# A time-mix layer with a GELU FFN on one core: the first loads in a written order, and the last block's tiles in earlier chunks

## The chip, the cores and the metric

The kernel runs on one core of a Trainium2 chip. The metric is the time in microseconds that the device takes for one execution; shorter is better. The core has engines that run side by side and wait for each other by semaphores: TensorE (PE in the profile, with its weight loads as PEld), VectorE (DVE), ScalarE (ACT), GpSimd (POOL) and SyncE (SP). SP computes nothing; its queue issues most of the kernel's DMAs. ACT can issue DMAs too, in the same queue as its own work.

## The reference

The input is x with 4 sequences of 1024 tokens of 512 channels. It is normalised, and the sum of x, a time-mix branch and an FFN branch is the output.

```python
xn = _layernorm(x)
# time mix
xx = concatenate([xn[:, 1:2, :], xn[:, :-1, :]], axis=1) - xn
k = einsum('btc,hc->bth', xn + xx * time_mix_k, Wk)      # HIDDEN = 704
r = einsum('btc,hc->bth', xn + xx * time_mix_r, Wr)
w = exp(-exp(time_decay))
state = state * w + relu(k_t);  out_t = state * r_t      # scan over t
out = einsum('bth,ch->btc', out, Wv)
out = (out - mean) * rsqrt(var + 1e-5) * ln_gamma + ln_beta
# FFN, N = 2048
D = gelu(dot(fp16(xn), W0.T) + bias0)                    # rounded to fp16
E = fp16(dot(D, W1.T) + bias1)
return x + out + E
```

## The kernel before, in words

The tokens are cut into 8 blocks of 512 (two to a sequence). A block is computed channel-major: `xnT` holds the transposed normalised block, and one tile is 128 partitions by 512.

*Precision.* Products that have to be near float32 are made of several passes in the fast float32 format: an operand is split into a truncated part, a rest, and a mixture (`split_x`, L281, `split_kr`, L238). Three passes with a scale S make one product (`three_pass`, L624): 8 matmuls into a bank `pa`, 4 into a bank `pb`, then ACT scales `pa` (L642), and DVE adds `pb` (L643). HIDDEN is 5 tiles of 128 and a half tile of 64 (`half_pass`, L653). Block 0, whose weights are still being split, uses plain float32 products (`raw_k`, `raw_r`, `raw_halves`).

*A block's loop.* For each block i, n runs over the 16 chunks of 128 rows of the FFN's hidden dimension N. A turn of n does, in PE's order: `up` for chunk n + 2 (L782, 8 matmuls, bank `pd`), `down` for chunk n (L810, 8 matmuls into the four accumulators `pe`, one for each row tile s of 128 tokens), and then the time-mix tiles that the dictionary `pieces` holds for that n. The work on ACT and DVE that follows a tile (relu, the scan over time, the gate with r, the splits of the gated result, the norm of an output tile) is run as a "follower" in the turn after it, woven with the background jobs `bg[n]` (weight fetches, splits, the next block's norm and transposes). For the blocks from 1 on, the five k tiles stand in chunks 0 to 4, the two halves in 5 and 6, the five r tiles in 7 to 11, and the four output tiles (`out_piece`, from the gated result and Wv) in 12 to 15. In the last block, the output tiles stand two to a chunk in 12 and 13 instead. The order of the PE, DVE, ACT and SP instructions within this loop is the written one (`manual_schedule`); elsewhere a planner of the framework orders the instructions.

*The last block's end.* There the down groups of the last 4 chunks (`tail = 4`) are left out of the loop. After the loop they are run for each row tile s by itself: tiles 0 and 1 into `pe` (L1022), tiles 2 and 3 by halves of the columns into fresh banks `end` (`end_by_columns`, L820), for which the sums of chunks 0 to 11 plus the bias have been put into `base` (L1016). Each is followed by a rounding (L769), an addition to the residual (L775) and a store of the output (L779).

*Weights and buffers.* Terms of Wk and Wr are written to DRAM once and fetched for each tile (`load_kr`, L275, three loads of 256 KB, name `kr`; 6 buffers, so two tiles' worth). W1's terms (`w`, 512 KB, 2 buffers) and W0's low terms (`w0l`, 256 KB, 3 buffers) are fetched for each chunk. All of these are on SP's queue, in the written order, where a load waits until its buffer is free. Most other tiles come from one common pool of 62 buffers (tag `q`), small scratch tiles from a ring of 6 (`temp`), PE's results from 4 banks (`bank`) and 4 more for `pe`.

*The start.* `load_x` (L100) issues the four row tiles of x's first block on SP, and the first three tiles of Wk in the middle of them (`amid`). ACT's queue issues the small loads: the two mix vectors (`mix_rows`), the decay in two parts and the FFN's bias (`late_rows`, 22 rows that are transposed on PE and become per-partition scalars). Three tiles of Wr follow on SP. These first loads are ordered by the planner. DVE clears a part of `late_rows` (L134), and the loads of its full rows come behind that. `first_inputs` (L389) then works out the first block by row tiles: the statistics and a square root on ACT (L416) for tile 0, the normalisation (L309), the transposes on PE (`turned`, L429), the mixing (`mixed_first`), and the first products (L387) of k. In PE's written order, the transpose of `mix_rows` (L462) comes behind 10 dummy products (L405) and ahead of the first transposes; the transpose of `late_rows` (L467) and one more dummy product stand between the first transposes and the first products.

Of the kernel before, what the change touches and what calls it, by code (L numbers as in the profile page):

```python
# [22 lines left out]
def time_mix_and_gelu_ffn(  # L23
# [69 lines left out]
    def bank(name):  # L93
        return ps_mm.tile([P, TB], F32, tag="mm", name=name)
# [2 lines left out]
        b, t0 = blocks[i]  # L97
        return b, slice(t0 + s * P, t0 + (s + 1) * P)

    def load_x(i, name, amid=lambda: None):  # L100
        xs = const.tile([P, NS, C], F32, tag="x", name=f"{name}_{i}")
        for s in range(NS):
            if s == NS // 2:
                amid()
            b, rows = tokens_of(i, s)
            nc.sync.dma_start(xs[:, s, :], x[b, rows, :])
        return xs
# [9 lines left out]
        src = sources[kind].rearrange("(c p) k -> p c k", p=P)  # L117
        nc.sync.dma_start(raw_w[kind, h], src[:, :, h * P : (h + 1) * P])

    x_now = load_x(0, "x", lambda: [load_raw(0, h) for h in range(FIRST)])  # L120
    ident = part("ident", F32)[:, :P]
    make_identity(nc, ident)
    nhalf = const.tile([P, NS], F32, name="nhalf")
# [7 lines left out]
    mk_sb, mr_sb = mix_sb[:, :NC], mix_sb[:, NC:]  # L131
    ND = NF + 1
    late_rows = part("late_rows", F32)[: ND + NN, :P]
    nc.vector.memset(late_rows[:, HF:], 0.0)  # L134
    late_sb = const.tile([P, ND + NN], F32, name="late_sb")
    w_sb, b0_sb = late_sb[:, :ND], late_sb[:, ND:]

    def rows_of(ap):
        return ap.rearrange("(c p) -> c p", p=P)

    nc.scalar.dma_start(mix_rows[:NC], rows_of(mix_k))
    nc.scalar.dma_start(mix_rows[NC:], rows_of(mix_r))
    nc.scalar.dma_start(late_rows[:NF], rows_of(decay[:H0]))
    nc.scalar.dma_start(late_rows[NF:ND, :HF], decay[H0:].rearrange("(c p) -> c p", p=HF))
    nc.scalar.dma_start(late_rows[ND:], rows_of(bias0))
    for h in range(FIRST):
        load_raw(1, h)
    raw_half = part("raw_half", F32).rearrange("p (two c k) -> p two c k", two=2, c=NC)
    gamma_sb = const.tile([P, C], F32, name="gamma_sb")
    beta_sb = const.tile([P, C], F32, name="beta_sb")  # L150
# [442 lines left out]

        return after

    def raw_halves(j, sums):
        for c in range(NC):
            for q, sum_ in enumerate(sums):
                rows = slice(q * HF, (q + 1) * HF)
                for out_, kind, src in (  # L600
                    (sum_[:HF], 0, xks[j, c]),
                    (sum_[HF:], 1, xrs[j, c]),
                ):
                    nc.tensor.matmul(  # L604
                        out_,
                        raw_half[rows, kind, c, :],
                        src[rows],
                        start=(c == 0),
                        stop=(c == NC - 1),
                    )  # L610

        def after():
            both = temp(f"kr_{j}")
            nc.scalar.copy(both, sums[0])
            nc.vector.tensor_add(both, both, sums[1])
            rk, st = temp(f"rk_{j}_{NF}"), temp(f"st_{j}_{NF}")
            nc.scalar.activation(rk[:HF], both[:HF], AF.Relu)
            yield
            scanned(j, NF, HF, st, rk)
            yield from gated_half(j, st, both[HF:])  # L620

        return after
# [250 lines left out]
    with tc.manual_schedule(engines=engines):  # L873
        for i in range(len(blocks)):
            j = i + 1
            tail = 4 if i == LAST else 0
            by_columns = range(NS // 2, NS) if tail else ()
            pieces, bg, early = {}, defaultdict(list), defaultdict(list)

            def put(n, fn, *args):  # L880
                bg[n].append(lambda: fn(*args))
# [14 lines left out]
            def turn(first, end):  # L896
                transposed(state["x"], first, end)

            for s in range(NS):
                pieces[12 + (s // 2 if i == LAST else s), s] = [out_piece, i, s]  # L900
            if i == 0:
                state["x"] = x_next
                pieces[1, 0] = [raw_k, i, 3]
                pieces[3, 0] = [raw_r, i, 3]
                pieces[5, 0] = [raw_k, i, 4]
                pieces[7, 0] = [raw_r, i, 4]
                pieces[9, 0] = [
                    lambda i: raw_halves(i, [bank(f"pkr_{i}_{q}") for q in range(2)]), i
                ]
                put(0, several, split_kr, (1, 0, 0), (1, 1, 0))  # L910
                put(0, several, split_w0, (1, 2), (1, 3))
                for c in range(NC):
                    put(2 + c - (c == 0), split_w0, 2, c)
                    put(3 + c, load_w0, 3, c)
                    put(5 + c, split_w0, 3, c)
                put(1, stats, *range(NS))
                put(3, lambda: norm_apply(j, state["x"]))
                for n, *which in ((1, 0, 1), (3, 0, 2), (5, 0, 3), (7, 0, 4), (7, 1, 1)):
                    put(n, split_kr, 1, *which)
                put(4, turn, 0, 1)  # L920
                put(5, turn, 1, 5)
                put(7, turn, 5, 10)
                put(8, turn, 10, 11)
                put(9, turn, 11, 16)
                put(9, load_late_constants)
                put(12, split_half)
                mix_at = (11, 12, 13, 15)
            else:
                order = [(0, h) for h in range(NF)] + [(1, h) for h in range(NF)]
                for k, (kind, h) in enumerate(order):  # L930
                    pieces[k + 2 * kind, 0] = [three_pass, i, kind, h]
                    if k > 1:
                        split_here = (kind, h) in raw_w
                        put(k - 2 + 2 * (k > 6) + split_here, fetch_kr, i, kind, h)
                pieces[5, 0] = [half_pass, i, 0]
                pieces[6, 0] = [half_pass, i, 1]
                for c, n in enumerate((2, 3, 4, 5) if i == 1 else (2, 2, 3, 3)):
                    put(n, split_xr, i, c)
                if j <= LAST:
                    put(1 if i == 1 else 2, fetch_x)  # L940
                    for s in range(NS):
                        put(2 + s // 2 if i == 1 else 4, stats, s)
                    put(4 if i == 1 else 5, lambda: norm_apply(j, state["x"]))
                    turns = (4, 6, 4, 2) if i == 1 else (4, 5, 4, 3)
                    for k in range(sum(turns)):
                        unit = next(n for n in range(4) if k < sum(turns[: n + 1]))
                        put(6 + unit, turn, k, k + 1)
                mix_at = (10, 12, 13, 15) if i == 1 else (10, 12, 13, 14)
            if i == 1:
                for g in range(NN // G):  # L950
                    put(4 * g, store_w0l, g)
                for h, n in enumerate((11, 12, 13, 13, 13, 15)):
                    put(n, split_wv, h)
            put(11 if j <= LAST else 2, fetch_residual)
            if j <= LAST:
                for c in range(NC):
# [9 lines left out]
            for n in range(NN):  # L966
                ahead = n + AHEAD
                if ahead == NN and j <= LAST:
                    xf = next_xf
                nxt = (i, ahead) if ahead < NN else (j, ahead - NN)  # L970
                gelu = up(*nxt) if nxt[0] <= LAST else None
                works = [follow() for follow in followers]
                works = [w for w in works if next(w, works) is None]
                several(scaled_now, *early[n])
                if i == 0 or n == NN - NS or (n > NN - NS and i < RAW_OUT):
                    finished(*works)
                    works = []
                followers = []
                if gelu:
                    d = gelu()  # L980
                if ahead + 1 == NN and j <= LAST:
                    next_xf = ffn_input(j)
                if n < NN - tail:
                    operands = waiting.pop(0)
                    for s in range(NS):
                        down(n, s, *operands, end=NN - tail if s in by_columns else NN)
                if gelu and i > 0:
                    waiting.append((d, load_w1(*nxt)))
                two_on = (i, ahead + 2) if ahead + 2 < NN else (j, ahead + 2 - NN)
                if two_on[0] <= LAST:  # L990
                    load_w0l(*two_on)
                jobs = [
                    lambda s=s: finish(i - 1, s, e16s[s])
                    for s in (2 * n, 2 * n + 1)
                    if s < len(e16s)
                ]
                for s in range(NS):
                    if (n, s) in pieces:
                        fn, *args = pieces[n, s]
                        followers.append(fn(*args))  # L1000
                if i == 0 and ahead + 1 < NN:
                    load_w1_raw(ahead + 1)
                woven(works, jobs + bg[n])
                if i == 0:
                    waiting.append((d, load_w1(*nxt)))
                store_weights()
# [60 lines left out]
```

## Time and profile before

| | us |
|---|---|
| median of 3 runs | 873.87 |
| lowest, highest | 873.59, 874.65 |
| the profiled execution's own time | 874.32 |
| span in its profile, from the first to the last instruction | 872.5 |
| PE busy | 861.3 |
| DVE busy | 669.7 |
| ACT busy | 431.1 |
| mean granted clock of TensorE | 0.997 |
| DMA, mean rate over the span | 225 GB/s |

The profile is of one execution. Its times count from the first instruction. A line of the timeline gives the start, the duration, the engine, the line of the program, the operation, and the result and operands; "x3" means that several like instructions are merged. The bracket at the end tells how long the engine had been idle and which instruction or DMA released it. An engine's name with a q (SPq, ACTq) is its queue, which issues DMAs; a DMA's duration there is that of the issue, and its landing is some microseconds later.

### The profile page before, as it was taken

What the parts mean: (1) busy time and instruction counts of PE and PEld (TensorE: products, weight loads), DVE (VectorE), ACT (ScalarE), POOL (GpSimd) and SP (SyncE); (2) the same over time, 40 slices, a digit from 0 to 9 for tenths busy, and PEclk for the clock granted to TensorE, in tenths of its full rate; (3) what the DMA queues carried; (4) which work ended last, traced back from release to release, by engine and by line L of the source; (5) the groups of instructions that cost most, each with busy time, mean ns of one, the idle gap of its engine ahead of it and who ended that gap; (6) DMA issues with size and microseconds to landing.
All of it is one profiled execution on the core that took longest, in us unless ns stands there. A gap on an engine that the chain in (4) does not pass through costs nothing.

```text
span 872.5 us, 11125 instructions
## 1 busy us (share of the span) xinstructions
PE 861.3 (99%) x3760; PEld 687.6 (79%) x3760; DVE 669.7 (77%) x1098; ACT 431.1 (49%) x733; POOL 73.8 (8%) x142
## 2 busy tenths in 40 slices
PE   8999999999999999999999999999999999999996
PEld 7677657887578888888888888888888888888885
DVE  4778876798777978778887888788886797864547
ACT  3866643456634464445625356254553446444430
POOL 1100000000011001000021001100011200200001
PEclk9999999999999999999999999999999999999998
DMA  8687946957568655877559666696756866577631
GB/s 261 224 279 264 335 169 207 313 173 254 184 223 276 224 186 181 287 243 236 177 171 335 208 214 198 208 320 205 223 195 218 306 192 226 181 234 280 232 122 50
DMA packets 101029, 196.59 MB, mean 225 GB/s; under 512 B 11087, under 2 KB 25452, under 8 KB 100972
## 3 DMA queue, kind: packets, MB, share of 16 engines
q1 hardware_dynamic: 100912, 195.86, 67.5%
q8 instruction: 30, 0.49, 0.2%
q14 instruction: 27, 0.22, 0.1%
q10 hardware_dynamic: 60, 0.02, 0.0%
HBM read 167.00 MB, written 28.84 MB: 224 GB/s over the span
## 4 chain that ended last, share of the span: by engine, by line
PE 97%; DVE 1%; DMA 1%; issue 0%; SPq 0%; ACTq 0%; ACT 0%; DVEq 0%
PE pd L790 27%; PE pe L812 26%; PE pa L630 15%; PE pb L387 7%; PE oa L727 6%; PE po L686 4%; PE ob L735 3%; PE ph L659 3%; PE pk L387 2%; PE pr L387 2%; PE ob L737 1%; DMA wk<-in_L_attn_Wk 1%; PE po L698 0%; PE pkr L604 0%; DVE xres L775 0%; PE pt L429 0%
## 5 line engine op out<-in xcount | busy, mean ns | idle before, releaser
L812 PE MATMUL pe<-w,d 128*128 128x512 f32 x1008 | 248.9, 389 | 0.0
L812 PEld LDWEIGHTS pe<-w,d 128*128 128x128 f32 x1008 | 189.1, 188 | 39.5
L790 PE MATMUL pd<-xf,w0h 128*128 128x512 f32 x512 | 203.5, 398 | 0.0
L790 PE MATMUL pd<-xf,w0l 128*128 128x512 f32 x512 | 199.3, 389 | 0.0
L800 ACT ACTIVATE d<-pd,late_sb 128x512 f16<-128x512 f32 x128 | 87.7, 685 | 161.5 <-PE pd L790 161.3
L790 PEld LDWEIGHTS pd<-xf,w0h 128*128 128x128 f32 x512 | 96.1, 188 | 25.8 <-issue 4.9
L790 PEld LDWEIGHTS pd<-xf,w0l 128*128 128x128 f32 x512 | 96.2, 188 | 21.7 <-issue 1.9
L643 DVE SCALAR_TENSOR_TENSOR y<-pb,a 128x512 f32<-128x512 f32 x70 | 48.4, 691 | 70.5 <-PE pb L387 69.5
L642 ACT ACTIVATE a<-pa 128x512 f32<-128x512 f32 x70 | 41.9, 598 | 86.3 <-PE pa L630 86.0
L805 ACT CAST d<-d 128x512 fp32r<-128x512 f16 x128 | 79.6, 622 | 4.0
L331 DVE STREAM_TRANSPOSE xnT<-x 32x512 f32<-32x512 f32 x112 | 78.6, 702 | 2.1
L630 PE MATMUL pa<-hk,kr 128*128 128x512 f32 x140 | 54.5, 389 | 0.0
L630 PE MATMUL pa<-lk,kr 128*128 128x512 f32 x140 | 54.5, 389 | 0.0
L299 POOL TENSOR_SCALAR ry<-mvy 128x1 f32<-128x1 f32 x32 | 16.5, 514 | 436.9 <-DVE mvy L306 436.9
L630 PE MATMUL pa<-hr,kr 128*128 128x512 f32 x128 | 49.8, 389 | 0.0
L630 PE MATMUL pa<-lr,kr 128*128 128x512 f32 x128 | 49.8, 389 | 0.0
L727 PE MATMUL oa<-wv,hg 128*128 128x512 f32 x120 | 46.7, 389 | 0.0
L727 PE MATMUL oa<-wv,lg 128*128 128x512 f32 x120 | 46.7, 389 | 0.0
L645 ACT ACTIVATE y<-y 128x512 f32<-128x512 f32 x35 | 22.2, 633 | 47.6 <-DVE y L643 47.6
L387 PE MATMUL pb<-mk,kr 128*128 128x512 f32 x140 | 37.4, 389 | 0.0
L686 PE MATMUL po<-wvraw,g 128*128 128x512 f32 x80 | 35.6, 592 | 0.0
L387 PE MATMUL pb<-mr,kr 128*128 128x512 f32 x128 | 34.2, 389 | 0.0
(166 smaller groups left out, 1322.3 us busy)
## 6 DMA issues: line engine op xcount, KB each, us to landing
w<-w1d SPq DMA_DIRECT2D x110, 512.0 KB, 3.7
kr<-krd SPq DMA_DIRECT2D x201, 256.0 KB, 4.9
w0l<-w0d SPq DMA_DIRECT2D x96, 256.0 KB, 4.3
x<-in_L_attn_x SPq DMA_DIRECT2D x32, 256.0 KB, 5.3
w1d<-w SPq DMA_DIRECT2D x16, 512.0 KB, 3.0
xres<-in_L_attn_x SPq DMA_DIRECT2D x32, 256.0 KB, 5.3
krd<-wt SPq DMA_DIRECT2D x30, 256.0 KB, 3.9
out<-xres SPq DMA_DIRECT2D x28, 256.0 KB, 5.2
```

What stands on the lines that cost most here:

```text
L331: nc.vector.transpose(dst[i * Q : (i + 1) * Q, :, :, j, :], src[j * Q : (j + 1) * Q, :, :, i, :],)
L387: return nc.tensor.matmul(dst, w[:, c, :], src, start=(c == 0), stop=(c == NC - 1))
L630: nc.tensor.matmul(pa, w[p][:, c, :], xs[j, c][p], start=(c == 0 and p == 0), stop=(c == NC - 1 and p == 1),)
L642: nc.scalar.activation(a, pa, AF.Copy, scale=1.0 + 1.0 / S)
L643: nc.vector.scalar_tensor_tensor(y, pb, -1.0 / S, a, ALU.mult, ALU.add)
L659: nc.tensor.matmul(pa, w[:, c].rearrange("p two k -> p (two k)"), xs[j, c][p], start=(c == 0 and p == 0), stop=(c == NC - 1 and p == 1),)
L686: nc.tensor.matmul(pos[s], gs[i, h][:, s * P : (s + 1) * P], wv_raw[h], start=(h == 0), stop=False,)
L727: nc.tensor.matmul(pa, gs[i, h][p][:, cols], wv[h][p], start=(h == 0 and p == 0), stop=(h == NF - 1 and p == 1),)
L790: nc.tensor.matmul(pd, w, xf[c], start=(c == 0 and p == 0), stop=(c == NC - 1 and p == 1),)
L800: nc.scalar.activation(d16, pd, AF.Gelu, bias=b0_sb[:, n : n + 1])
L805: nc.scalar.copy(d, d16)
L812: nc.tensor.matmul(pe[s] if sum_ is None else sum_, d[:, s * P : (s + 1) * P], w1[p][:, cols], start=(n == first and p == 0), stop=(n == e ...
```

## The change

There are two parts.

*The loads.* The order of the first loads on SP and ACT is now a written one. ACT's queue keeps the two mix loads and has them first. The decay and bias loads go to SP's queue. `load_x` takes one list of loads for each row tile, which are issued ahead of that tile: SP's order is x tiles 0 and 1, three tiles of Wk, x tile 2, the three small row loads, x tile 3, three tiles of Wr. `late_rows` is cleared by GpSimd instead of VectorE.

*The last block.* The k, r, half and output tiles get their chunks from lists. For the last block, the k tiles move from chunks 0, 1, 2, 3, 4 to 0, 1, 2, 2, 3, the halves from 5, 6 to 3, 4, the r tiles from 7 to 11 to 4 to 8, and the output tiles from 12, 12, 13, 13 to 9, 10, 11, 11. The fetch of the weights' terms for tile k stays right behind tile k - 2, wherever that is; the splits of the r input move from chunks 2, 2, 3, 3 to 1, 2, 2, 3. In chunks 12 and 13 only `up` for chunks 14 and 15 is left. A chunk's entry in `pieces` may now hold several works. For the other blocks the lists give the same chunks as before.

```diff
-    def load_x(i, name, amid=lambda: None):
+    def load_x(i, name, amid=()):
         xs = const.tile([P, NS, C], F32, tag="x", name=f"{name}_{i}")
         for s in range(NS):
-            if s == NS // 2:
-                amid()
+            for load in amid[s : s + 1]:
+                load()
             b, rows = tokens_of(i, s)
             nc.sync.dma_start(xs[:, s, :], x[b, rows, :])
         return xs
...
-    x_now = load_x(0, "x", lambda: [load_raw(0, h) for h in range(FIRST)])
...
-    nc.vector.memset(late_rows[:, HF:], 0.0)
+    nc.gpsimd.memset(late_rows[:, HF:], 0.0)
...
-    nc.scalar.dma_start(mix_rows[:NC], rows_of(mix_k))
-    nc.scalar.dma_start(mix_rows[NC:], rows_of(mix_r))
-    nc.scalar.dma_start(late_rows[:NF], rows_of(decay[:H0]))
-    nc.scalar.dma_start(late_rows[NF:ND, :HF], decay[H0:].rearrange("(c p) -> c p", p=HF))
-    nc.scalar.dma_start(late_rows[ND:], rows_of(bias0))
-    for h in range(FIRST):
-        load_raw(1, h)
+    def load_late_rows():
+        nc.sync.dma_start(late_rows[:NF], rows_of(decay[:H0]))
+        nc.sync.dma_start(
+            late_rows[NF:ND, :HF], decay[H0:].rearrange("(c p) -> c p", p=HF)
+        )
+        nc.sync.dma_start(late_rows[ND:], rows_of(bias0))
+
+    with tc.manual_schedule(engines={nc.sync.engine, nc.scalar.engine}):
+        nc.scalar.dma_start(mix_rows[:NC], rows_of(mix_k))
+        nc.scalar.dma_start(mix_rows[NC:], rows_of(mix_r))
+        x_now = load_x(
+            0,
+            "x",
+            (
+                lambda: None,
+                lambda: None,
+                lambda: [load_raw(0, h) for h in range(FIRST)],
+                load_late_rows,
+            ),
+        )
+        for h in range(FIRST):
+            load_raw(1, h)
...
-            for s in range(NS):
-                pieces[12 + (s // 2 if i == LAST else s), s] = [out_piece, i, s]
+
+            full_at = [0, 1, 2, 3, 4, 7, 8, 9, 10, 11]
+            half_at, out_at = [5, 6], [12, 13, 14, 15]
+            if i == LAST:
+                full_at = [0, 1, 2, 2, 3, 4, 5, 6, 7, 8]
+                half_at, out_at = [3, 4], [9, 10, 11, 11]
+
+            def piece(n, *work):
+                pieces[n].append(work)
+
...
                 for k, (kind, h) in enumerate(order):
-                    pieces[k + 2 * kind, 0] = [three_pass, i, kind, h]
+                    if k == NF:
+                        for half in range(2):
+                            piece(half_at[half], half_pass, i, half)
+                    piece(full_at[k], three_pass, i, kind, h)
                     if k > 1:
                         split_here = (kind, h) in raw_w
-                        put(k - 2 + 2 * (k > 6) + split_here, fetch_kr, i, kind, h)
-                pieces[5, 0] = [half_pass, i, 0]
-                pieces[6, 0] = [half_pass, i, 1]
-                for c, n in enumerate((2, 3, 4, 5) if i == 1 else (2, 2, 3, 3)):
+                        put(full_at[k - 2 + split_here], fetch_kr, i, kind, h)
+                xr_at = {1: (2, 3, 4, 5), LAST: (1, 2, 2, 3)}.get(i, (2, 2, 3, 3))
+                for c, n in enumerate(xr_at):
                     put(n, split_xr, i, c)
...
+            for s, n in enumerate(out_at):
+                piece(n, out_piece, i, s)
...
-                if i == 0 or n == NN - NS or (n > NN - NS and i < RAW_OUT):
+                if i == 0 or n == out_at[0] or (n > out_at[0] and i < RAW_OUT):
                     finished(*works)
                     works = []
...
-                for s in range(NS):
-                    if (n, s) in pieces:
-                        fn, *args = pieces[n, s]
-                        followers.append(fn(*args))
+                for work, *args in pieces[n]:
+                    followers.append(work(*args))
```

More of the change, by code (lines that the diff above doesn't have):

```diff
@@ L594, in raw_r, with raw_halves @@
         return after
-    def raw_halves(j, sums):
+    def raw_halves(j):
+        sums = [bank(f"pkr_{j}_{q}") for q in range(2)]
         for c in range(NC):
@@ L877, in time_mix_and_gelu_ffn @@
             by_columns = range(NS // 2, NS) if tail else ()
-            pieces, bg, early = {}, defaultdict(list), defaultdict(list)
+            pieces, bg, early = defaultdict(list), defaultdict(list), defaultdict(list)
             def put(n, fn, *args):
@@ L897, in turn @@
                 transposed(state["x"], first, end)
-            for s in range(NS):
-                pieces[12 + (s // 2 if i == LAST else s), s] = [out_piece, i, s]
+            full_at = [0, 1, 2, 3, 4, 7, 8, 9, 10, 11]
[5 more added lines that the diff above has]
+                pieces[n].append(work)
             if i == 0:
                 state["x"] = x_next
[L903 to L909, printed above, removed]
+                piece(1, raw_k, i, 3)
+                piece(3, raw_r, i, 3)
+                piece(5, raw_k, i, 4)
+                piece(7, raw_r, i, 4)
+                piece(9, raw_halves, i)
                 put(0, several, split_kr, (1, 0, 0), (1, 1, 0))
```

## The prediction

> **What bounds the kernel now.** I read the page first (busy shares), then the chain of waits, then the timeline of the first 30 us and of the last 18 us, last the timeline of block 7's first chunks on PE and SP.
>
> ```profile
> span 872.5 us, 11125 instructions
> ...
> PE 861.3 (99%) x3760; PEld 687.6 (79%) x3760; DVE 669.7 (77%) x1098; ACT 431.1 (49%) x733; POOL 73.8 (8%) x142
> ```
>
> PE is busy for 861.3 of 872.5 us; the 11.2 us left lie at the two ends. From 10.22 to 864.55 us the timeline shows no idle PE: up (L790) and down (L812) groups follow each other at 1.81 us for 8 matmuls, 0.227 us each. So order in the middle is worth nothing unless it makes PE wait; only an earlier start or a shorter end pays.
>
> The chain of waits begins with a load:
>
> ```profile
> 2.11 4.58 DMA wk<-in_L_attn_Wk
> 10.43 3.53 PE pk L387 x18
> ```
>
> Timeline at the start (start, duration, engine, line, in brackets the idle time before and its releaser):
>
> ```profile
> 3.22 0.26 ACTq L142 DMA_DIRECT2D mix_rows<-in_L_attn_time_mix_r  x1
> ...
> 6.71 0.33 ACTq L145 DMA_DIRECT2D late_rows<-in_L_ffn_bias  x1
> 6.71 0.18 PEld L462 LDWEIGHTS small<-ident,mix_rows 8*128 8x128 f32 x1 [1.65 <-issue]
> ...
> 7.08 0.29 ACT L416 ACTIVATE rx<-mvx,eps_sb 128x1 f32<-128x1 f32 x1 [4.87 <-DMA wk<-in_L_attn_Wk]
> ...
> 7.61 0.74 DVE L309 TENSOR_SCALAR x<-x,mvx,rx 128x128 f32<-128x128 f32 x2
> ...
> 9.41 0.17 PEld L467 LDWEIGHTS small<-ident,late_rows 22*128 22x128 f32 x1 [0.51 <-ACT xk L439]
> ...
> 9.63 0.80 PE L405 MATMUL idle<-const-float32-0.0 128*128 128x128 f32 x2
> ...
> 10.22 3.73 PE L387 MATMUL pk<-xk,wk 128*128 128x128 f32 x18
> ```
>
> ACT's first square root (L416) stands behind the issue of the bias load (L145), which itself waits for a wk load to land (6.69). The statistics it needs were done at 4.13. That is one wait of 2.9 us. There is a second one behind it: PE transposes late_rows (L467) in its queue ahead of the first products (L387), and the bias row landed at 9.19 (6.71 plus the 2.5 us to landing that its tile shows). The products follow that transpose and one dummy pair, 0.6 us later for their weight load (10.01).
>
> Timeline at the end:
>
> ```profile
> 856.93 3.79 PE L812 MATMUL pe<-w,d 128*128 128x512 f32 x16
> 857.21 0.69 DVE L742 SCALAR_TENSOR_TENSOR oy<-ob,oa 128x512 f32<-128x512 f32 x1 [2.54 <-PE ob L737]
> ...
> 858.42 0.67 DVE L1016 TENSOR_TENSOR base<-pe,b_sb 128x512 f32<-128x512 f32 x1
> ...
> 860.56 3.99 PE L812 MATMUL end<-w,d 128*128 128x256 f32 x32
> ...
> 862.31 0.69 DVE L769 TENSOR_TENSOR e<-pe,b_sb 128x512 f16<-128x512 f32 x1
> ...
> 869.54 0.42 DVE L775 TENSOR_TENSOR xres<-xres,e 128x256 f32<-128x256 f32 x1
> ```
>
> PE ends at 864.55, DVE at 869.97: DVE has 12.76 us of work, without a gap, behind the last output tile, and PE gives it only 7.6 us of cover (856.93 to 864.55). The last store then takes until 871.7. So the end is DVE's.
>
> **What the Trainium skill says.** (1) "TensorE: Matmul & The Clock Gate", its table of specifications: ScalarE's and VectorE's queues are strict FIFO. The trace agrees: L416 sat idle 4.87 us behind a load that it doesn't need. (2) "DMA: Bandwidth & Descriptors", Queues, rings and completion order: each issuing queue has its own ring on each of the 16 engines, read in ring order, rings in turn. So a small load on SP's ring comes after all that SP issued earlier. The trace agrees on order in SP's ring: three kr terms of block 7 land some 0.65 us apart in order of issue. (3) The first page, Part 1: PE runs at half clock until a window of about 3.4 us is busy, and the window is free-running. Here the first products take 421 ns up to 13.2 us and 275 ns from 14 us on.
>
> **The change, part by part.**
>
> *Loads.* ACT keeps the two mix loads. Its square root can start when the statistics are done, about 4.1 (the memset of late_rows, 0.11 us, goes from DVE to idle POOL). The reciprocal is behind the statistics of row tile 1 (4.27 to 4.97), so it runs at about 5.0 instead of 7.41; the normalisation, the transposes and the first mix move by 2.4 us. mix_rows was landed at 6.7 because its second load was issued at 3.22; issued at about 1.4 it lands about 4.0 (the first one took 1.46 to 4.04), and PE is in its dummies until 5.36 anyway. So without late_rows the first products could start when the mix is ready, 7.6, with the third wk at 7.79 (issued 2.66, 5.1 to landing).
>
> The three row loads go on SP behind x tile 2 and ahead of x tile 3. A load also waits for the landing of the one that had its completion semaphore before, eight in turn: that is why L145 waited for wk, x tile 3 for wk (issued 5.84), wr for wk (7.80). With mix, x, x, wk and x tile 2 as the first eight, the rows wait for the mix loads and x tile 0 (3.2 to 4.0), x tile 3 for x tile 1 (4.25), wr for wk (5.82). SP issued x tile 2 at 3.21 (0.53) and it landed at 8.40 (5.2). The rows are then issued between 3.7 and 5.0 (0.26 to 0.50 each) and, in ring order, land right after it: 8.45 to 8.7. From the bias's landing to the products' weight load before: 9.19 to 10.01, 0.82. So 8.55 + 0.82 = 9.4: gain 0.6 us. Bounds: 0 if they land behind x tile 3 (9.35 before), 2.2 if they slip past (products at 7.85). The clock: if the window closes at 13.49 as before, an earlier start only runs cold longer, and of 0.6 some 0.3 are kept; if PE's shorter pauses let a window close early, the 15 products that ran cold (10.22 to 13.4) take 0.112 instead of 0.213 us, 1.5 in all. I take 0.6. x tile 3 (needed at 16.0) and wr (needed at 24.15) are issued earlier, 4.8 and 5.9 instead of 5.84 and 7.80; nobody waits for them. All behind the start is PE-bound and shifts whole.
>
> *Last block, chunks 0 to 4.* Up, down and three-pass groups keep their number; only their order changes. Two k tiles in chunk 2 mean that the terms for k tile 3, fetched when k tile 1 leaves its buffers, are used one chunk earlier:
>
> ```profile
> 776.33 1.91 SPq L278 DMA_DIRECT2D kr<-krd  x3
> ```
>
> They landed at 781.41, 782.06 and 782.70 by the semaphores' records; k tile 2 ends at 782.59, which becomes the start of k tile 3. Weight loads run 0.2 us ahead, so the slack is 1.0, 0.55 and 1.5 us. K tile 4 starts 6.35 us later (788.93) and its terms landed by 788.18: 0.7 us or more. The residual's four loads on SP now stand behind six kr loads, and w1 for chunk 5 is issued when its buffer is free (788.97) as before. The xr splits (1.8 us of DVE each) are one chunk earlier and needed at 797.1; by DVE's timeline they end by 790. Four banks are held by chunk 2's tiles, and the next up group needs the first: ACT read pa at 781.88 to 782.48, needed at 785.3. All hidden: 0. If the kr terms took the 7.3 us of the chunk 0 fetch, PE would lose 1.7 and 0.7.
>
> *The end.* Before, behind the last output tile (856.93) PE has 7.62 us; after, up 14 and 15 as well, 3.63 more, 11.25. Chunk 15's d comes from ACT after up 15: 0.26 + 0.69 + 0.03 + 0.62 = 1.6 us behind it, while PE has 6 matmuls (1.36) to do first, and the weight load of d isn't prefetched: a new stall of 0.45. DVE has the same 13.04 us from that point to its end (856.93 to 869.97); the PE bound is 11.25 + 0.45 + 0.9 (read, add) = 12.6. DVE still ends last: 13.04, from a point 3.63 earlier: gain 3.6. If the two bases (1.2) are placed ahead: 12.6, gain 4.05. If e of tile 0 keeps its place (5.4 behind the point) its sum is there only at 6.2: 0.8 lost, gain 2.8. The stores' tail is unchanged (1.75).
>
> **Sum.** 0.6 + 3.6 = 4.2 us against the profiled execution's 874.32 (span 872.5 and 1.8 around it): 870.1. The median of the runs is 0.45 lower, so 869.7.
>
> **Rivals.**
> A, as above: 869.7, own range 868.6 to 870.9.
> B, late_rows don't bind. For: they are 2.5 to 8 KB beside 256 KB. Against: decay, issued at 4.33 on ACT's own ring, landed at about 8.2, no earlier than its neighbours. Gain 2.2 + 3.6 = 5.8, with the clock 7.3: 866.6 to 868.1.
> C, the end is less and the start nothing: rows behind x tile 3, e of tile 0 in place: 2.8, 871.1.
> D, slower. Chunks 2 to 4 of the last block hold 16 w0h, 17 wv, 12 xk, 12 xr and 4 g tiles, 61 of the 62 buffers of the common pool. If one more is wanted than there are, DVE stands at the scan (L523) until k tile 4 frees one, and ACT's gelu behind it; one chunk of PE's period (6.35) less 4.2 makes it 2.1 slower, 876.0. It decides from the 63rd buffer. For: the count is one short. Against: xk leaves two chunks earlier too.
> E, kr terms late by the 2.4 above, start nothing, end 2.8: 0.4 gained, 873.5.
>
> **How the numbers follow.** A 0.52, B 0.16, C 0.16, E 0.08, D 0.08. A measurement of this kernel tells about 0.2%, 1.75 us, from no change; so faster is A, B and C, 0.84, same E, 0.08, slower D, 0.08. The range 867.0 to 871.8 holds A, C and most of B.
>
> **What would show it.** L416 near 4.2; L467's weight load between 8.6 and 8.9, and L387 at 9.3 to 9.6; PE without idle time from there; a pause of 0.4 to 0.5 us in the first pe group behind up 15; DVE ending about 1.3 us behind PE instead of 5.4. Wrong if L467 waits past 9.2, if PE waits at L630 in the last block, or if DVE has gaps behind L742.

## The result, and the profile after

| | before | after |
|---|---|---|
| median of the runs, us | 873.87 (5 runs, 873.40 to 874.65) | 869.98 (5 runs, 869.78 to 870.18) |
| ratio, with its 95% interval | | 0.9954 [0.9939, 0.9968] |
| the profiled execution's own time | 874.32 | 869.99 |
| its span | 872.5 | 868.2 |
| PE ends, DVE ends | 864.55, 869.97 | 863.88, 865.62 |

The kernel became 3.9 us faster in medians. The two profiled executions differ by 4.33 us, and that is the sum to be taken apart. First the page of the kernel after (busy time, share, instructions):

```profile
span 868.2 us, 11132 instructions
...
PE 860.8 (99%) x3760; PEld 686.9 (79%) x3760; DVE 669.8 (77%) x1097; ACT 431.1 (50%) x733; POOL 74.4 (9%) x143
```

The same work is there: PE has its 3760 matmuls and nearly the same busy time (860.8 us, before 861.3), DVE has one instruction less and POOL one more (the memset). What shrank is time in which PE had nothing, at the two ends. The timeline of the start of the kernel after (start, duration, engine, line, operation; in brackets the idle time before and what released it):

```profile
3.64 0.69 DVE L428 BATCH_NORM_STATS2 stx<-x 128x6 f32<-128x512 f32 x1 [2.76 <-DMA x<-in_L_attn_x]
...
4.58 0.29 ACT L430 ACTIVATE rx<-mvx,eps_sb 128x1 f32<-128x1 f32 x1 [1.49 <-DVE mvx L429]
4.59 0.32 SPq L145 DMA_DIRECT2D late_rows<-in_L_ffn_bias  x1
...
5.63 0.94 PE L443 MATMUL pt<-ident,x 128*128 128x128 f32 x4
...
8.65 0.21 PE L481 MATMUL small<-ident,late_rows 22*128 22x22 f32 x1 [2.09 <-DMA late_rows<-in_L_ffn_bias]
...
9.17 3.54 PEld L401 LDWEIGHTS pk<-xk,wk 128*128 128x128 f32 x18
9.38 3.53 PE L401 MATMUL pk<-xk,wk 128*128 128x128 f32 x18
...
12.74 0.60 PE L443 MATMUL pt<-ident,x 128*128 128x128 f32 x4
```

(The new line numbers for those of before: L416 is now L430, L462 and L467 are L476 and L481, L387 is L401, L429 is L443.) The square root no longer waits for a load: it is released by its own statistics, at 4.58 instead of 7.08, and the first transposes begin 2.4 us earlier, at 5.63. But PE then stands 2.09 us in front of the transpose of `late_rows`, and the bracket names the bias. So the products' weight load is only 0.84 us earlier (10.01 to 9.17), and the second row tile's transposes 1.05 us (13.79 to 12.74). This 1.05 to 1.10 is found again at every later mark up to the last block, in this pair of profiled executions. The chain of waits of the kernel after says the same from the other side (start, length, piece):

```profile
4.59 3.93 DMA late_rows<-in_L_ffn_bias
8.52 0.14 issue
8.65 0.21 PE small L481
8.86 0.73 PE idle L419 x2
9.59 3.32 PE pk L401 x18
```

In the chain of before, a load of wk stood in this place; now it is the last of the three small loads.

The end, in the timelines of DVE and of PE:

```profile
852.49 0.69 DVE L757 SCALAR_TENSOR_TENSOR oy<-ob,oa 128x512 f32<-128x512 f32 x1 [3.16 <-PE ob L752]
...
856.93 0.75 DVE L734 SCALAR_TENSOR_TENSOR oy<-oy,ry,beta_sb 128x512 f32<-128x512 f32 x1
857.71 0.69 DVE L735 TENSOR_TENSOR xres<-xres,oy 128x512 f32<-128x512 f32 x1
858.32 0.75 DVE L734 SCALAR_TENSOR_TENSOR oy<-oy,ry,beta_sb 128x512 f32<-128x512 f32 x1
859.10 0.69 DVE L735 TENSOR_TENSOR xres<-xres,oy 128x512 f32<-128x512 f32 x1
859.71 0.68 DVE L784 TENSOR_TENSOR e<-pe,b_sb 128x512 f16<-128x512 f32 x1
860.43 0.69 DVE L790 TENSOR_TENSOR xres<-xres,e 128x512 f32<-128x512 f32 x1
...
865.20 0.42 DVE L790 TENSOR_TENSOR xres<-xres,e 128x256 f32<-128x256 f32 x1
```

```profile
855.84 4.22 PE L827 MATMUL pe<-w,d 128*128 128x512 f32 x16
859.89 3.99 PE L827 MATMUL end<-w,d 128*128 128x256 f32 x32
```

Before, DVE did the operations from 856.93 on in this order:

```profile
861.65 0.75 DVE L719 SCALAR_TENSOR_TENSOR oy<-oy,ry,beta_sb 128x512 f32<-128x512 f32 x1
862.31 0.69 DVE L769 TENSOR_TENSOR e<-pe,b_sb 128x512 f16<-128x512 f32 x1
862.91 0.69 DVE L720 TENSOR_TENSOR xres<-xres,oy 128x512 f32<-128x512 f32 x1
863.51 0.75 DVE L719 SCALAR_TENSOR_TENSOR oy<-oy,ry,beta_sb 128x512 f32<-128x512 f32 x1
864.18 0.69 DVE L775 TENSOR_TENSOR xres<-xres,e 128x512 f32<-128x512 f32 x1
```

The last output tile's matmuls now end at 852.21 instead of 856.93: 4.72 us earlier, of which 3.63 are the two `up` groups (for chunks 14 and 15) that now come behind it and 1.09 the start. Call this point, where PE goes on from the last output tile to other work, the hand-over. From there DVE needs 13.41 us (865.62 less 852.21), where it needed 13.04. So the end gives 3.63 - 0.37 = 3.26, and with the start's 1.09 that makes 4.35, against 4.33 measured. DVE still ends last, 1.74 us behind PE instead of 5.4.

PE's 16 matmuls into `pe` take 4.22 us where they took 3.79. The view of the waits of the last block says for what (engine, place, what it waits for: us, times, longest):

```profile
PEld pe L827 <- ACT d L820: 0.6, 1, 0.6
```

It is chunk 15's `d`, once. It costs no time yet, since DVE ends last.

### The profile page after: what moved, and what is told of

Same layout as the page of the kernel before. It is cut to its first block, busy times and chain, and to the rows that moved or that the text cites. A ratio compares the mean times of both kernels' runs of the same rounds, so it can differ in the third digit from the quotient of the medians.

```text
span 868.2 us, 11132 instructions
## 1 busy us (share of the span) xinstructions
PE 860.8 (99%) x3760; PEld 686.9 (79%) x3760; DVE 669.8 (77%) x1097; ACT 431.1 (50%) x733; POOL 74.4 (9%) x143
## 4 chain that ended last, share of the span: by engine, by line
PE 97%; DVE 1%; DMA 0%; SPq 0%; issue 0%; DVEq 0%
PE pd L805 26%; PE pe L827 26%; PE pa L645 15%; PE pb L401 7%; PE oa L742 6%; PE po L701 4%; PE ob L750 3%; PE ph L674 3%; PE pk L401 2%; PE pr L401 2%; PE ob L752 1%; PE po L713 0%; DMA late_rows<-in_L_ffn_bias 0%; PE pkr L619 0%; DVE xres L790 0%; DVE e L784 0%
## 5 line engine op out<-in xcount | busy, mean ns | idle before, releaser
L401 PE MATMUL pb<-mk,kr 128*128 128x512 f32 x140 | 37.4, 389 | 0.0
L757 DVE SCALAR_TENSOR_TENSOR oy<-ob,oa 128x512 f32<-128x512 f32 x24 | 16.6, 692 | 24.9 <-PE ob L752 24.9
```

Of the source, the lines that this page charges most:

```text
L401: return nc.tensor.matmul(dst, w[:, c, :], src, start=(c == 0), stop=(c == NC - 1))
```

## The experiments

Each was timed in turn with the kernel before on the same chip, and has a ratio to it. The edits of e3 to e10 are made to the changed kernel.

### The two parts by themselves

e1 is the kernel before with only the part of the change that concerns the loads, e2 the kernel before with only that which concerns the last block. Of each, the core of the diff against before:

```diff
-    nc.scalar.dma_start(late_rows[ND:], rows_of(bias0))
+        nc.sync.dma_start(late_rows[ND:], rows_of(bias0))
```

```diff
+            if i == LAST:
+                full_at = [0, 1, 2, 2, 3, 4, 5, 6, 7, 8]
+                half_at, out_at = [3, 4], [9, 10, 11, 11]
```

> The kernel before with the new order of the first loads alone, the last block as before. Theory (the two parts add up, and everything between them is bound by TensorE): the first products start 0.8 us earlier and the clock rises 1.3 us earlier, so the first row tile ends 1.05 us earlier and the whole run is 1.05 us shorter: ratio about 0.9988 to before. Rival (the start is absorbed by a later wait, and the last block brings all of the 4.3 us): ratio 1.000.

Measured: 874.31 against 874.45 (13 and 17 runs), ratio 0.9998 [0.999, 1.0006]. The 1.05 us didn't come.

> The kernel before with the last block's earlier tiles alone, the first loads as before. Theory: VectorE ends 3.63 us of TensorE time earlier, less 0.37 us that its own order costs: 3.3 us shorter, ratio about 0.9962. Rival (the last block's tiles cost stalls in chunks 2 to 4 that only the earlier start hides): less than 2.5 us. A stall of 0.4 us in the first pe group behind the last up group is expected by both.

Measured: 871.53 (869.77 to 871.74), ratio 0.9962 [0.9949, 0.9974]: 2.9 us by the medians, 3.3 by the ratio, where 3.3 was expected. In its profile the end is that of the changed kernel (13.41 us from the hand-over at 853.76 to 867.17), and PE has no wait in block 7's earlier chunks. So the last block does by itself what it does in the sum; in this execution all that follows the start came 0.46 us later than in before's profile, where the clock rose at 13.49; here it rose for good only at 14.85.

Why e1 gave nothing is seen in the timeline of its start and in its windows (busy time of PE, PEld, DVE, ACT, POOL; then the granted clock of PE, the DMA share and GB/s):

```profile
8.88 0.26 PE L481 MATMUL small<-ident,late_rows 22*128 22x22 f32 x1 [2.36 <-DMA late_rows<-in_L_ffn_bias]
...
9.67 4.05 PE L401 MATMUL pk<-xk,wk 128*128 128x128 f32 x18
...
13.51 0.77 PE L443 MATMUL pt<-ident,x 128*128 128x128 f32 x4
```

```profile
core 0: us, PE busy (x) PEld busy (x) DVE busy (x) ACT busy (x) POOL busy (x), PEclk, DMA share, GB/s
3.60:7.00 3.40, 2.01 (x14) 1.37 (x12) 2.92 (x11) 1.45 (x7) 0.79 (x2) 1.00 0.99 297
7.10:13.80 6.70, 4.92 (x23) 4.90 (x24) 2.28 (x8) 2.00 (x5) 0.79 (x2) 0.50 0.95 279
```

The products begin 0.55 us earlier than before (10.22 to 9.67), but all 18 run at half clock, and the next transposes come only 0.28 us earlier (13.79 to 13.51). The clock had been raised at 3.60; then PE stood still in front of `late_rows`, and the clock fell again for 6.8 us. In the changed kernel's profile the fall lasts only from 8.80 to 12.21:

```profile
5.40:8.80 3.40, 1.16 (x7) 0.64 (x7) 2.99 (x13) 1.45 (x6) 0.79 (x2) 1.00 1.04 328
8.90:12.20 3.30, 3.30 (x16) 3.30 (x17) 0.42 (x2) 1.87 (x4) 0.80 (x2) 0.50 0.95 274
12.30:15.00 2.70, 2.70 (x26) 2.66 (x25) 1.55 (x6) 1.14 (x4) 0.00 (x0) 1.00 0.97 326
```

The windows' edges fall differently in each execution, and the mean granted clock of every timed run shows it: 9 of e1's 13 runs have 0.993 or 0.994 and take 873.9 to 875.4 us, the other 4 have 0.995 or 0.996 and take 873.0 to 873.5. (This mean also takes in a lower clock at the very end, behind PE's last work.) So what the loads alone are worth depends on where the clock's window lies, and in time it could not be told from nothing.

e0 is the changed kernel once more, beside e5 to e7.

> The changed kernel itself once more, as the common base of these four. Expected: 869.8 to 870.6; its start moves by up to 1.5 us from execution to execution with the phase of the clock's window, so the middle value can differ by some tenths from the first measurement.

Measured: 869.92 (869.71 to 870.96), ratio 0.9951 [0.9939, 0.9964]. Its loads and the changed kernel's are e1's, yet nine of these ten runs lie between 869.71 and 870.18; why e1 met the longer fall of the clock so much oftener isn't shown.

### The start: what do the rows hold up?

e3 moves the transpose of `late_rows` behind the second row tile's transposes, and the work of ACT that reads it one turn later.

```diff
             turned(0)
-            nc.tensor.transpose(late_t, late_rows, ident[: ND + NN, : ND + NN])
             busy(1)
...
                         turned(s + 1)
+                        if s == 0:
+                            nc.tensor.transpose(
+                                late_t, late_rows, ident[: ND + NN, : ND + NN]
+                            )
                     products(c, cols)
-                if s == 0:
+                if s == 1:
                     nc.scalar.copy(late_sb, late_t)
```

> The changed kernel with the transpose of late_rows (and ScalarE's work on it) taken out of the way of the first products: behind the transposes of row tile 1, the work on ScalarE behind row tile 1's mixing. Theory (the bias row's landing at 8.5 holds the first products, and the pause it makes lets the clock fall): products at 7.1 to 7.5 instead of 9.2, the clock stays up, transposes of row tile 1 at about 9.3 instead of 12.7: 3.4 us shorter than the changed kernel, about 866.6. Half theory (rows hold the products, but the clock falls as before): 1.5 to 2 us shorter. Rival (ScalarE's square root and the mixing set the start): no change, 870.

Measured: 866.84, ratio 0.9914 [0.99, 0.9927]; 3.1 us below the changed kernel. The timeline of its start:

```profile
6.73 0.68 PE L401 MATMUL pk<-xk,wk 128*128 128x128 f32 x4 [0.25 <-ACT xk L453]
7.74 1.80 PE L401 MATMUL pk<-xk,wk 128*128 128x128 f32 x14 [0.33 <-DMA wk<-in_L_attn_Wk]
9.38 0.60 PE L443 MATMUL pt<-ident,x 128*128 128x128 f32 x4
9.91 0.24 PE L493 MATMUL small<-ident,late_rows 22*128 22x22 f32 x1
```

The first products come at 6.73 instead of 9.38, and there is now a short wait for the third wk, which the rows had hidden. The second transposes come 3.36 us earlier than in the changed kernel. No window falls: the clock is full from 3.70 on. So it was the rows that held the start; the first products don't read them, and what reads them (ACT's copy and exponential) can come a row tile later at no cost that the profile shows.

e4 leaves the wait where it is and fills the pause with dummy products, so that only the clock changes.

```diff
             turned(0)
+            busy(9)
             nc.tensor.transpose(late_t, late_rows, ident[: ND + NN, : ND + NN])
```

> The changed kernel with nine more dummy products between the first transposes and the transpose of late_rows, which fill TensorE's pause (6.4 to 8.6 us) and compute nothing that is used. Theory (the pause inside one window of 3.4 us lets the clock fall at 8.8, and the first 13 products run at half speed): products start at about 9.1 as before but take 0.11 us each, so the run is 1.3 to 1.6 us shorter than the changed kernel, about 868.5. Rival (the clock rises and falls by a phase of its own): no change, 870, or worse by the dummies' time if they push past the landing.

Measured: 868.53, ratio 0.9937 [0.9924, 0.9949], as expected by the median; four of its five runs lie between 868.20 and 868.59, and one took 870.42 with a clock of 0.999, for which there is no profile. Two lines of its timeline:

```profile
9.05 2.17 PE L401 MATMUL pk<-xk,wk 128*128 128x128 f32 x18
11.06 0.60 PE L443 MATMUL pt<-ident,x 128*128 128x128 f32 x4
```

The 18 products take 2.17 us instead of 3.53. So, by the medians, some 1.45 of e3's 3.1 us are the clock (869.98 to 868.53), and the other 1.7 the wait itself (868.53 to 866.84).

e8 asks whether SP's queue was the right place for the rows: it issues them on ACT's again, straight behind the two mix loads.

```diff
-        nc.sync.dma_start(late_rows[:NF], rows_of(decay[:H0]))
+        nc.scalar.dma_start(late_rows[:NF], rows_of(decay[:H0]))
...
         nc.scalar.dma_start(mix_rows[NC:], rows_of(mix_r))
+        load_late_rows()
...
-                load_late_rows,
```

> The changed kernel with the three row loads back on ScalarE's queue, but in the written order, straight behind the two mix loads and ahead of all of ScalarE's work. It tells which half of the edit counts, the queue or the order. Theory (a load's place ahead of the large ones counts, whoever issues it): the rows land by 5 us, the products start when mixing and the third Wk tile allow, 7.2 to 8.0, and the clock mostly stays up: 1.5 to 3 us shorter than the changed kernel, 867 to 868.5. Rival (the loads' completion semaphores, eight in turn, are used up by the small loads, so that Wk's second and third tile wait for the mix loads and land later): 869 to 870.

Measured: 868.02 (866.99 to 869.55), ratio 0.9934 [0.9922, 0.9947]. The time lies within what the theory expected, but the timeline shows the rival's wait:

```profile
6.54 0.49 PE L419 MATMUL idle<-const-float32-0.0 128*128 128x128 f32 x2
6.92 0.46 PE L401 MATMUL pk<-xk,wk 128*128 128x128 f32 x2
...
8.26 0.49 PE L401 MATMUL pk<-xk,wk 128*128 128x128 f32 x2 [0.88 <-DMA wk<-in_L_attn_Wk]
9.15 3.27 PE L401 MATMUL pk<-xk,wk 128*128 128x128 f32 x14 [0.40 <-DMA wk<-in_L_attn_Wk]
```

The rows were there by 5.1 and no longer bind. Now SP's second and third wk do: they were issued at 3.51 and 3.92 instead of 2.17 and 2.72, and landed at 8.21 and 9.01. The view of the waits has for SP's queue:

```profile
SPq L118 <- DMA x<-in_L_attn_x: 1.4, 1, 1.4
```

With five small loads on ACT's queue, x, x and the first wk, the eight completion semaphores are used up, so the second wk waited for a landing before it was issued: by the trace's semaphore records it has the semaphore of the first x tile, which landed at 3.49 (the rival had named the mix loads). So this written order lets the rows be early and makes wk late. It is still 2.0 us faster than the changed kernel, so the rows' place there did cost time; but e3, which leaves every load where it is, gains 3.1. The rows at the head of SP's own queue weren't tried. The profiled run is the slowest of the five and had its clock lowered from 8.83 to 12.24; three of the others have a mean clock of 1.0 (866.99 to 868.02).

### The end: what does DVE have behind the last output tile?

e5 works out the two bases in chunk 11, ahead of the last output tiles.

```diff
+    def early_base(s):
+        bases[s] = part(f"base_{s}", F32)
+        nc.vector.tensor_add(bases[s], pe[s], b1_sb)
...
+            if i == LAST:
+                for s in by_columns:
+                    put(11, early_base, s)
...
-        bases = {}
-        for s in by_columns:
-            bases[s] = temp(f"base_{s}")
-            nc.vector.tensor_add(bases[s], pe[s], b1_sb)
```

> The changed kernel with the two bases (1.25 us of VectorE) computed in chunk 11, where VectorE has nothing else to do, instead of behind the last output tile. Theory (VectorE's work behind the last output tile, 13.4 us, sets the end, and TensorE's 11.7 plus one rounding, addition and wait, 1.0, is next): 0.7 us shorter, then TensorE-bound. Rival (the end is set by TensorE's own tail already): no change, within 0.2 us.

Measured: 868.98, ratio 0.9941 [0.9928, 0.9953]; 0.94 less than e0 in medians, and 0.78 in the profile: from the hand-over to DVE's end it is 12.62 us (851.95 to 864.57) instead of 13.40 in e0.

e6 adds to e5 an order in which PE needn't wait for `d`: chunks 12 to 14 of row tiles 0 and 1 ahead of chunk 15 of both.

```diff
+        for s in range(NS // 2):
+            for n, operands in chunks[:-1]:
+                down(n, s, *operands)
         for s in range(NS):
...
-                for n, operands in chunks:
+                for n, operands in chunks[-1:]:
                     down(n, s, *operands)
```

> As the kernel with early bases, and row tiles 0 and 1 both take chunks 12 to 14 before either takes chunk 15, so that TensorE has 2.7 us of matmuls instead of 1.4 while ScalarE makes chunk 15's d. Theory: the 0.40 us stall goes, and as the end is TensorE's by then, another 0.4 us: 1.1 us shorter than the changed kernel. Rival (VectorE still ends last with early bases): as the kernel with early bases.

Measured: 870.02, ratio 0.9954 [0.9941, 0.9968]: no gain over the changed kernel, 1.0 us worse than e5. The timeline of the end of e6:

```profile
856.38 3.79 PE L827 MATMUL pe<-w,d 128*128 128x512 f32 x16
...
859.75 0.69 DVE L784 TENSOR_TENSOR e<-pe,b_sb 128x512 f16<-128x512 f32 x1 [0.34 <-PE pe L827]
```

PE's stall is gone (3.79 us), but the sum of row tile 0 is finished later, and DVE, which is the engine that ends last, now waits 0.34 us for it. From the hand-over (852.75) to DVE's end (865.67) it is 12.92, 0.30 more than in e5. The hand-over itself is 0.80 later than in e5: 0.55 of it from the start, where the window of the lower clock ended later (12.73 against 11.73), and 0.19 from chunk 2 of block 7, where the weight load at 782.10 waited for a load of `kr`. The theory failed by the rival's mechanism: it took time off PE, which didn't bind, and gave it to DVE, which did.

### Sums of edits

> All that helped or should: late_rows' transpose behind row tile 1, early bases, and the order of the end. Theory (start and end add up): 866.8 less 1.1, about 865.7. Rival (one of the three was only worth something where another bound stood): 866.3 or more.

e7 has the edits of e3, e5 and e6. Measured: 866.29, ratio 0.9908 [0.9894, 0.9921]. The end again takes 12.93 us (849.03 to 861.96), as in e6; the rival's time held.

> Rows' transpose behind row tile 1 and early bases, TensorE's end as in the changed kernel. Theory (the order of the end that was tried cost 0.3 us, since row tile 0's sum came later and VectorE waited for it): 0.3 us shorter than all three together (866.3), 866.0. Rival (that order was neutral): 866.3.

e10 has those of e3 and e5 alone. Measured: 866.2, ratio 0.9911 [0.9897, 0.9924], with 12.62 us at the end. The medians of e7 and e10 can't be told apart; the ends in the profiles differ by the 0.3 us of the theory.

e9 adds to e10 a half of e6's order, only chunk 12 of row tile 1 ahead of chunk 15 of row tile 0, and puts the last output norm's two additions behind both of the operations that they read, instead of each right behind its own.

```diff
         nc.vector.scalar_tensor_tensor(y, y, rstd, beta_sb, ALU.mult, ALU.add)
+        if i == LAST:
+            yield
         nc.vector.tensor_add(z, z, y)
...
+        for s, some in ((0, chunks[:-1]), (1, chunks[:1])):
+            for n, operands in some:
+                down(n, s, *operands)
...
-                for n, operands in chunks:
+                for n, operands in (chunks[-1:], chunks[1:])[s]:
```

> Rows' transpose behind row tile 1, early bases, and two mendings of the end: row tile 1's chunk 12 alone stands between row tile 0's chunk 14 and 15 (it hides 0.45 us of the 0.40 us stall and delays row tile 0's sum by 0.05 only), and the last block's output norm alternates its two row tiles at the last addition too, so that no addition stands right behind the operation that it reads. Theory (VectorE's work behind the last output tile then takes 12.3 instead of 13.4 us, TensorE's 11.3 plus 0.9): 1.1 us shorter than with the rows' move alone, 865.7. Rival: as with the other order of the end, 866.3.

Measured: 866.04, ratio 0.991 [0.9896, 0.9923]. Its DVE at the end:

```profile
853.82 1.41 DVE L737 SCALAR_TENSOR_TENSOR oy<-oy,ry,beta_sb 128x512 f32<-128x512 f32 x2
855.14 1.29 DVE L740 TENSOR_TENSOR xres<-xres,oy 128x512 f32<-128x512 f32 x2
856.35 0.68 DVE L789 TENSOR_TENSOR e<-pe,b_sb 128x512 f16<-128x512 f32 x1
```

The four operations take 2.53 us (853.82 to 856.35), in e5 2.78 (855.75 to 858.53). The end takes 12.24 us, the least of all (12.3 was expected). But the hand-over is 0.79 us later than in e10's profile: 0.28 from the start, where the third wk kept PE waiting 0.45 us, and 0.49 from a wait for a load of `w` at 157 us. e7, e9 and e10 can't be told apart in time; all three lie 3.7 to 3.9 us below the changed kernel's median, and most of it is e3's edit.

## Why the prediction was right, and where its terms were off

The forecast was 869.7, and 870.1 for the profiled execution; it came to 869.98 and 869.99. Of its sum, two terms were off in opposite directions.

- *The square root.* Its wait went as said. It runs at 4.58, not 4.1, since x tile 0 itself was there 0.4 us later (statistics at 3.64 instead of 3.22). Nothing hung on it, since the rows came later still.
- *The rows in SP's order.* Issued from 3.9, landed at 8.52 (8.45 to 8.7 was said); L481's weight load at 8.62 (8.6 to 8.9 was said), products at 9.38 (9.3 to 9.6). Rival B, that they don't bind, falls by the bracket of 2.09 us, and e3 shows what it would have been worth. Rival C needed them behind x tile 3, with no gain at the start, and falls too. One reading was too strict, that a small load comes after all that SP issued earlier: by the semaphore records the smallest of the three (0.2 KB, issued at 4.32) landed at 7.60, ahead of x tile 2 (issued at 3.27, landed at 8.13). The other two landed behind it, and so the last of them set the time.
- *The start's size: 0.6 said, 1.05 to 1.10 in the profile.* The step that failed is "from the bias's landing to the products' weight load before: 9.19 to 10.01, 0.82". In before's profile the bracket of L467 names ACT's xk, not the bias, so this interval had a part that belongs to ACT's mixing. From the landing it is 0.65 (8.52 to 9.17). That makes 0.84 of the gain. The other 0.2 is the clock: 9.38 to 12.74 is 3.36 us, where 10.22 to 13.79 was 3.57, because the window at half speed ended at 12.21, not at 13.49. The text had bounded the clock, but kept the rule "if the window closes at 13.49 as before"; what it missed is that the pause of 2.1 us could lower a clock that the dummies had already raised. e4 puts the price of that at 1.45 us, and e1 shows that it can take the whole gain.
- *Chunks 0 to 4 cost nothing.* Right: PE has no idle time there. K tile 3 started at 781.49, and its terms had landed at 780.00, 780.63 and 781.28; the weight loads that first read them came 1.3, 0.9 and 1.8 us later, where 1.0, 0.55 and 1.5 had been worked out. There is no wait at the scan. Rivals D and E fall. The margin is thin all the same: e6's profile lost 0.19 us to just such a load.
- *The new stall.* 0.45 us was said. The gap between two matmuls of the `pe` group is 0.520 instead of 0.227 at 856.97, the next 0.335, so 0.40.
- *The end's size: 3.6 said, 3.26 measured.* The step that failed is "DVE has the same 13.04 us from that point to its end". The same operations took 13.41. Before, DVE's operations of the residual and of the rounding alternated, and all but the last two neighbours didn't depend on each other: from L719 at 861.65 in eight steps to 866.71 it is 5.06 us, each step 0.60 to 0.67 but for the one that depends, which is 0.72. After, each addition stands right behind the operation that it reads: the same eight steps, 856.93 to 862.36, take 5.43. A step onto such a reader takes 0.72 to 0.78 us in the fences above (856.93 to 857.71, 859.71 to 860.43), one onto an independent operation 0.61 (857.71 to 858.32). e9 got 0.25 of it back by the order alone. So DVE ends 1.74 us behind PE, where 1.3 had been said. The bound of 12.6 us that was worked out for PE is what e5 shows: DVE's end at 12.62, with its last rounding held by PE for 0.1 us (the last matmul ends at 863.65, the rounding starts at 863.69).

So the mechanisms of the two gains were right, and the total was nearer than its parts: +0.45 at the start, -0.34 at the end. That the two nearly cancel is luck. By the parts alone the forecast would look less exact: e2 gives 2.9 us and e1 0.1. The start's gain is read from one pair of profiles. How much of the changed kernel's 3.9 us the loads contribute in time stays open, between 0.1 (e1) and about 1.0 (what is left of 3.9 after e2's 2.9): the intervals of the changed kernel and of e2 overlap, and the clock moves the start of either from run to run.

## What to carry to other kernels

When a load is taken out of one wait, look for the next instruction in the written order that needs a load, and move that instruction rather than the load: here one transpose moved by a few lines gave 3.1 us, where the whole change had given 3.9. Read an interval in a profile from the releaser that the bracket names, not from the landing that seems to be its cause. At a tail that one engine ends, count starts to starts, since the same operations take longer when each reads the one just before.

## What the runs showed of the hardware

*A pause shorter than the window lowered the clock.* The Trainium skill, "TensorE: Matmul & The Clock Gate", Part 1, says that the clock falls after an idle window of about 3.4 us and rises after a busy one, and that the window is free-running. The records agree on its length (3.41 us between changes) and on the free phase: it rose first at 3.60 in e1, 3.70 in e3, 5.38 in the changed kernel and 13.49 before. They differ on the fall: a window needn't be idle. It fell after windows in which PE was busy for 34% (changed kernel, 5.38 to 8.79), 59% (e1, 3.60 to 7.01) and 70% (e8), and held after 67% (e10), 75% (e3) and more. The lines of e8, where the clock fell behind the window, and of e10, where it held:

```profile
5.41:8.82 3.41, 2.39 (x12) 1.53 (x12) 2.60 (x12) 3.07 (x10) 0.79 (x2) 1.00 0.95 267
```

```profile
3.71:7.12 3.41, 2.29 (x16) 1.73 (x16) 2.93 (x11) 1.60 (x7) 0.79 (x2) 1.00 1.02 306
```

Before, a window of 73% (up to 3.25) had not raised it, in e1 83% did. Between 67 and 75% the busy share of the trace doesn't decide it, and e2 has one window of 99% that left it low:

```profile
8.02:11.44 3.42, 3.37 (x14) 2.79 (x15) 2.87 (x12) 2.77 (x7) 0.79 (x2) 0.50 0.79 220
```

So this share isn't what the hardware counts; what it counts stays open. That the pause was the cause in the changed kernel is shown by e4, which fills it and changes nothing else: its five runs have a mean clock of 0.999 or 1.0, the changed kernel's 0.997 or 0.998. In the profiles of e3, e4, e7, e9 and e10, where no pause after the dummies was over 0.81 us, the clock never fell in the start; in e8, with one of 0.88, it did. Two numbers so close set no threshold. The times of such kernels often lie closer together, but not always: e3's five runs within 0.34 us, e4's five within 2.2, e1's thirteen within 2.4.

*Small loads aren't quick.* The bias, 8 KB, took 3.93 us from issue to landing on SP behind x and wk (4.59 to 8.52), where the first x tile of 256 KB was there 2.9 us after its issue (0.72 to 3.64).

*A load can wait for one eight places earlier.* In e8, five small loads moved ahead on ACT's queue delayed the issue of the second and third wk on SP's by 1.3 and 1.2 us. The profile names the landing of x as what SP waited for. The semaphore records of the trace say why: this program's loads carry eight completion semaphores in turn, so the ninth load, the second wk, has that of the first x tile, and it was issued at 3.51, right behind that tile's landing at 3.49. No run changed their number.
